# Two-layer graph network on one core: p spread through DRAM, projections one or two strips earlier, both norms scaled on ScalarE

## The chip, the cores and the metric

The kernel runs on one core of one Trainium2 chip. The metric is the device time of one execution in microseconds; the median of several runs is compared. Engines are called by the names of the profile: PE (matrix multiply), PEld (its weight load), DVE or VectorE, ACT or ScalarE, POOL or GpSimd, SP (the queue that issues most DMAs).

## The reference

There are 16 graphs ("batches") of 1024 nodes with 256 features, and two layers. Every layer adds its result to its input and normalises each row.

```python
# layer 0; adj holds 0 and 1 in these inputs, so of the four kinds only e0 is used
e0 = leaky(einsum('bid,bjd->bij', h * a0[:, 0], h))          # leaky slope 0.2
alpha = sigmoid(where(adj == 1, e0, -inf))
x = layernorm(x + einsum('bij,bjd->bid', alpha, h) + bias)
# layer 1
Hh = einsum('bni,io->bno', x, W);  s = Hh @ a_src;  d = Hh @ a_dst
e = where(adj != 0, exp(-leaky_relu(s[:, :, None] + d[:, None, :])), 0)
x = layernorm(x + elu(einsum('bnm,bmo->bno', e, Hh) / rowsum(e)))
```

## The kernel before

A batch is held as 8 tiles of 128 rows. The work of a batch falls into three stages on PE, and the program of each engine is in the order in which the code is written (no scheduler moves anything). In the main loop, iteration `b` does layer 0 of batch `b` and layer 1 of batch `prev = b - 1`, and stores batch `done = b - 2`.

**The strip stage.** Layer 0's scores are symmetric, so only the strips on and above the diagonal are computed: `strip(b, jt)` multiplies (tile `pe`, L198) and has 8, 7, ... 1 blocks of 128 columns for `jt` = 0 to 7. ACT takes two tanh of `pe` (`tb` L206, `low` L207), VectorE takes their maximum (L208), `finish` writes the row of `al` (L214) and POOL adds the diagonal (L224). `tb` has four buffers and `low` two. The lower half comes through DRAM: `dump` turns 32 x 32 blocks on VectorE (L230) and writes `tb` out on SP's queue (`mir`, L234), `gather` reads it back in columns (L238), and `mask(b, t)` on VectorE applies the adjacency to it (L244). Masks 0 to 2 stand after strips 5 to 7, masks 3 to 6 in the first sum. Between the strips stand the eight projections of the batch before: `project(prev, t)` (tile `pH`, L343), from which ACT makes `H` and, by an exponential, the two columns `pq` (L351 to L353), p and q of each node. In the main loop projection `t` stands after strip `t`; for the first batch they stand later.

`spread_p` (L355 to L363) lays p, which is a column, along the free axis on all 128 partitions: for each of eight tiles PE transposes the column repeated 128 times (`pp`, L362), and ACT copies two times 512 columns to `p` (L363).

**The first sum.** `sum0(b, t)`: eight `al` x `x` products for each of eight row tiles (`acc`, L294), then on VectorE the eviction (L302) and the row statistics (`st`, `mv`, L264 and L265). After four tiles POOL computes `r`, the inverse deviation (`rstd`, L271 to L279). VectorE then subtracts the mean and multiplies by `r` (`scale`, L283): for the first four tiles in slots 5 and 6, for the last four in the second sum. The scaled rows go to DRAM and back in blocks (`save_x1`, `fetch_x1`), and `turn_x1` on VectorE (L331) makes of them what `project` reads. In the same slots VectorE makes the weights of layer 1, `weights(prev, t)` (`e`, L375), one of eight per slot: a row tile of `e` from `p`, `q` and the adjacency. `scale1(done, t)` scales a tile of the output on VectorE, also by L283. ACT has four checks of the adjacency here (`junk`, L116). At the end POOL issues the load of a later adjacency (L102).

**The second sum.** `sum1`: eight `e` x `H` products per row tile (`acc`, L382), then `elu` on VectorE and ACT (L397 to L403) and `add` with its statistics on VectorE. The tail, after the loop, ends the last batch; there the output is scaled on ACT instead (`center` and `scale1_act`, L425), with POOL making the product of mean and `r`, negated (`mr`).

`ps_acc`, the pool of `acc` and `pH` in PSUM, has three buffers, `ps_e` of `pe` three, `ps_t` of `pp` two. `p` and `H` have one buffer each.

Of the kernel before, what the change touches and what calls it, by code (L numbers as in the profile page):

```python
# [18 lines left out]
P = 128  # L19
# [10 lines left out]
def one_kind_pass(  # L30
# [236 lines left out]
    def rstd(mv, what):  # L267

        n_t = mv.shape[1]
        ve = small.tile([P, NT], F32, tag="ve", name=f"ve_{what}")[:, 0:n_t]  # L270
        nc.gpsimd.tensor_scalar(ve, mv[:, :, 1], EPS, None, ALU.add)  # L271
        r = small.tile([P, NT], F32, tag="r", name=f"r_{what}")[:, 0:n_t]
        nc.gpsimd.tensor_tensor(r, ve, power[:, 0:n_t], ALU.pow)  # L273

        n = small.tile([P, NT], F32, tag="n", name=f"n_{what}")[:, 0:n_t]
        nc.gpsimd.tensor_tensor(n, r, r, ALU.mult)
        nc.gpsimd.tensor_tensor(n, n, ve, ALU.mult)
        nc.gpsimd.tensor_scalar(n, n, -0.5, 1.5, ALU.mult, ALU.add)
        nc.gpsimd.tensor_tensor(r, r, n, ALU.mult)  # L279
        return r  # L280

    def scale(y, mv, r):
        nc.vector.tensor_scalar(y, y, mv[:, 0:1], r, ALU.subtract, ALU.mult)  # L283

    x1s, mv0s, r0s = {}, {}, {}

    def sum0(b, t):
        if t == 0:
            x1s[b] = two.tile([P, NT, D], F32, tag="x1", name=f"x1_{b}")
            mv0s[b] = small.tile([P, NT, 2], F32, tag="mv0", name=f"mv0_{b}")  # L290
            r0s[b] = {}
        acc = ps_acc.tile([P, D], F32, tag="acc", name=f"acc0_{b}_{t}")
        for jt in range(NT):
            nc.tensor.matmul(  # L294
                acc,
                lhsT=als[b][:, jt, ts(t, P)],
                rhs=xs[b][:, jt, :],
                start=(jt == 0),
                stop=(jt == NT - 1),
            )  # L300
        y = x1s[b][:, t, :]
        nc.vector.scalar_tensor_tensor(y, acc, 0.5, bias_bc, ALU.mult, ALU.add)  # L302
        stats(y, mv0s[b][:, t, :], f"0_{b}_{t}")
        if t % HT == HT - 1:
            g = t // HT
            r0s[b][g] = rstd(mv0s[b][:, ts(g, HT), :], f"0_{b}_{g}")

    def scale0(b, t):
        scale(x1s[b][:, t, :], mv0s[b][:, t, :], r0s[b][t // HT][:, t % HT : t % HT + 1])


    x1Ts, Hs, pqs, p_bcs, es = {}, {}, {}, {}, {}
# [42 lines left out]
    def spread_p(b, g):  # L355

        if g == 0:
            p_bcs[b] = one.tile([P, N], F32, tag="p", name=f"p_{b}")
        pt = ps_t.tile([P, HT, P], F32, tag="t", name=f"pp_{b}_{g}")
        for t in range(HT):  # L360
            col = pqs[b][:, g * HT + t, 0:1]
            nc.tensor.transpose(pt[:, t, :], col.to_broadcast([P, P]), ident)  # L362
        nc.scalar.copy(p_bcs[b][:, ts(g, HALF)], pt.rearrange("p t q -> p (t q)"))  # L363

    def check_pq(b):
        near = small.tile([P, NT, 2], F32, tag="near", name=f"near_{b}")
        nc.vector.tensor_scalar(near, pqs[b], LOW, 1.0 / LOW, ALU.max, ALU.min)
        nc.vector.tensor_tensor(near, near, pqs[b], ALU.is_equal)
        nc.vector.tensor_reduce(fit[:, b : b + 1], near, AX.XY, ALU.min)
# [6 lines left out]
            es[b][:, m, :], p_bcs[b], pqs[b][:, m, 1:2], adjs[b][:, m, :], ALU.mult, ALU.min  # L376
        )

    hs, ys, mv1s, r1s, rms = {}, {}, {}, {}, {}

    def sum1(b, t, acc, m):
        nc.tensor.matmul(  # L382
# [26 lines left out]
        nc.vector.scalar_tensor_tensor(y, y, -1.0, x1s[b][:, t, :], ALU.add, ALU.add)  # L409
        stats(y, mv1s[b][:, t, :], f"1_{b}_{t}")  # L410

    def center(b, t0, n):

        mv = mv1s[b][:, ds(t0, n), :]
        r = rstd(mv, f"1_{b}_{t0}")
        mr = small.tile([P, NT], F32, tag="mr", name=f"mr_{b}_{t0}")[:, 0:n]
        nc.gpsimd.tensor_tensor(mr, mv[:, :, 0], r, ALU.mult)
        nc.gpsimd.tensor_scalar(mr, mr, -1.0, None, ALU.mult)
        for t in range(n):
            rms[b, t0 + t] = r[:, t : t + 1], mr[:, t : t + 1]  # L420

    def scale1_act(b, t):
        y = ys[b][:, t, :]
        r, mr = rms[b, t]
        nc.scalar.activation(y, y, AF.Identity, bias=mr, scale=r)  # L425

    def scale1(b, t):
        scale(ys[b][:, t, :], mv1s[b][:, t, :], r1s[b][:, t : t + 1])

    def store(b, t0, n):  # L430
        rows = out[b].rearrange("(t p) d -> p t d", p=P)
# [2 lines left out]
    def acc1(b, t, pool, tag):  # L434
        return pool.tile([P, D + 1], F32, tag=tag, name=f"acc1_{b}_{t}")
# [36 lines left out]
    for b in range(1, B):  # L472
        prev, done = b - 1, b - 2
        last = b == B - 1

        projects = [[jt] for jt in range(NT)]
        if prev == 0:

            projects = [[], [], [], [0, 1], [2, 3], [], [4, 5], [6, 7]]
        for jt in range(NT):  # L480
            strip(b, jt)
            if prev == 0 and jt in (1, 2):
                scale0(0, 2 * jt + 2)
                scale0(0, 2 * jt + 3)
            if prev == 0 and jt == 2:
                save_x1(0, 1)
                fetch_x1(0, 1)
            if prev == 0 and jt in (2, 5):
                turn_x1(0, (jt - 2) // 3)
            finish(b, jt)  # L490
            if jt < NT - 1:
                dump(b, jt)
            if jt >= 1:
                gather(b, jt - 1)
            for t in projects[jt]:
                project(prev, t)
            if jt >= 5:
                mask(b, jt - 5)
        for g in range(2):
            spread_p(prev, g)  # L500
        check_pq(prev)
        if not last:
            load_x(b + 1)
            new_xT(b + 1)
            load_blocks(xTs[b + 1], x[b + 1], 0, N)

        for t in range(NT):
            if 1 <= t < 5:
                mask(b, t + 2)
            weights(prev, t)  # L510
            if done >= 0:
                scale1(done, t)
                if t in (3, 7):
                    store(done, t - 3, HT)
            sum0(b, t)
            if t in (5, 6):
                scale0(b, 2 * t - 10)
                scale0(b, 2 * t - 9)
            if t == 6:
                save_x1(b, 0)  # L520
            if t >= NT - CHECKS:
                check_adj(b, t - NT + CHECKS)
        if not last:
            load_adj(b + 1)


        for t in range(NT):
            acc = acc1(prev, t, ps_acc, "acc")
            for m in range(NT):
                sum1(prev, t, acc, m)  # L530
            if last and t == 6:
                turn_x1(b, 1)
            if last and t == 7:
                weights(b, 0)
                weights(b, 1)
            elu(prev, t, acc)
            if t >= 1:
                add(prev, t - 1)
            if t == 0:
                fetch_x1(b, 0)  # L540
            if t in (1, 2):
                scale0(b, 2 * t + 2)
                scale0(b, 2 * t + 3)
            if t == 2:
                save_x1(b, 1)
            if t == 4:
                fetch_x1(b, 1)
                turn_x1(b, 0)
            if not last and t in (3, 5):
                turn_x(b + 1, (t - 3) // 2)  # L550
            if last and t in (5, 6):
                for n in range(HT):
                    project(b, (t - 5) * HT + n)
                spread_p(b, t - 5)
        if not last:
            turn_x1(b, 1)
            add(prev, NT - 1)
            r1s[prev] = rstd(mv1s[prev], f"1_{prev}")


    last, done = B - 1, B - 2
    first = [acc1(last, t, ps_e, "e") for t in range(3)]
    for m in range(NT):
        if m >= 2:
            weights(last, m)
        if m == 3:
            add(done, NT - 1)
            center(done, 0, NT)
        for t in range(3):
            sum1(last, t, first[t], m)  # L570
    check_pq(last)
    for t in range(NT):
        if t < 3:
            acc = first[t]
        else:
            acc = acc1(last, t, ps_acc, "acc")
            for m in range(NT):
                sum1(last, t, acc, m)
        elu(last, t, acc)
        if t in (3, 6):  # L580
            center(last, t - 3, 3)
        add(last, t)
        if t == 6:
            center(last, 6, 1)
        for q in range(2 * t - 6, 2 * t - 4) if 3 <= t < 7 else []:
            scale1_act(done, q)
            if q in (3, 7):
                store(done, q - 3, HT)
        if t == 6:
            for q in range(3):  # L590
                scale1_act(last, q)
            store(last, 0, 3)
    for q in range(3, 7):
        scale1_act(last, q)
        if q == 5:
            store(last, 3, 3)
    center(last, 7, 1)
    scale1_act(last, 7)
    store(last, 6, 2)


# [389 lines left out]
```

## Time and profile before

| | |
|---|---|
| median of 3 runs | 1329.43 us (1328.62 to 1329.67) |
| the profiled execution | 1330.3 us, span 1328.4 us, granted clock 0.992 |
| busy: PE, PEld, DVE, ACT, POOL | 1280.3, 1037.4, 1019.5, 546.5, 243.4 us |
| L382, L294, L198, L343 (PE) | 448.7, 448.5, 269.4, 133.0 us |
| L362 `pp` on PE, x128 | 20.5 us busy, mean 280 ns; 14.6 us idle before it |
| L363 copy of `p` on ACT, x32 | 17.1 us, mean 588 ns |
| L375 `e` on DVE, x128 | 162.8 us, mean 1275 ns |
| L283 scalings on DVE, x112 and x128 | 45.6 and 45.3 us, mean 408 and 396 ns |
| L425 scaling on ACT, x16 | 8.6 us, mean 596 ns |
| L102 `adj` issue on POOL, x34 | mean 800 ns; 1024 KB land in 13.6 us (median) |

A group of the page is a line with an engine: how often it ran, its busy time, the mean of one, and the idle time of its engine just before it with what ended that. A matmul's duration of 380 ns is longer than its place on PE, since matmuls are pipelined: 128 of them take 27.64 us in the chain. The chain follows what ended last back from the end; a wait says how long an engine stood, and for whom.

### The profile page before, as it was taken

The numbers are of one execution on the slowest core, as the hardware profiler recorded it, in microseconds if no ns is written. First come the engines' busy times: TensorE is split into PE (matmuls) and PEld (weight loads), VectorE is DVE, ScalarE is ACT, GpSimd is POOL, SyncE is SP. The second block draws the span as 40 slices with busy tenths as digits, with TensorE's granted clock in tenths as the row PEclk, the third lists the DMA queues.
The fourth block names the chain that finished last, engine by engine and source line by source line (L and its number), as shares of the span: only waits on it lengthen the run. The fifth ranks groups of instructions, "written<-read, shape, count | busy, mean of one in ns | idle before, by whom it ended". The sixth has DMA issues, their size and how long they took to land.

```text
span 1328.4 us, 17516 instructions
## 1 busy us (share of the span) xinstructions
PE 1280.3 (96%) x5550; PEld 1037.4 (78%) x5550; DVE 1019.5 (77%) x2318; ACT 546.5 (41%) x1236; POOL 243.4 (18%) x486
## 2 busy tenths in 40 slices
PE   7879999999999999999999999999999999999995
PEld 5758788687887878788687887878778687787874
DVE  5576886968869687886878869687886878869764
ACT  3352452715336162452715336162451624427034
POOL 2111111211112122111211112122111211112113
PEclk9999999999999999999999999999999999999998
DMA  9265687575677756687575677856686565775211
GB/s 215 54 133 113 109 174 143 113 164 104 145 141 157 160 103 150 109 180 143 111 162 106 150 138 152 162 105 151 111 177 130 110 151 106 172 143 111 68 29 66
DMA packets 606516, 173.36 MB, mean 130 GB/s; under 512 B 485584, under 2 KB 590928, under 8 KB 606416
## 3 DMA queue, kind: packets, MB, share of 16 engines
q1 hardware_dynamic: 580144, 137.56, 48.0%
q0 software_dynamic: 17952, 33.56, 14.8%
q10 hardware_dynamic: 8320, 1.05, 0.5%
q8 instruction: 46, 0.75, 0.2%
q14 instruction: 54, 0.44, 0.1%
HBM read 144.57 MB, written 61.08 MB: 155 GB/s over the span
## 4 chain that ended last, share of the span: by engine, by line
PE 83%; DVE 6%; DMA 3%; ACT 3%; SPq 2%; ACTq 1%; issue 1%; POOL 0%; DVEq 0%; POOLq 0%
PE acc L294 32%; PE acc L382 32%; PE pe L198 13%; PE pH L343 5%; DMA mir<-tb 2%; SPq L234 2%; DVE tb L208 1%; DVE al L214 1%; ACTq L110 1%; DVE tb L230 1%; ACT tb L206 1%; PE pp L362 1%; ACT low L207 1%; DVE st L264 1%; DVE y L409 0%
## 5 line engine op out<-in xcount | busy, mean ns | idle before, releaser
L382 PE MATMUL acc<-H,e 128*128 128x257 f32 x2048 | 448.7, 380 | 1.6 <-DVE e L375 1.6
L294 PE MATMUL acc<-x,al 128*128 128x256 f32 x2048 | 448.5, 381 | 0.0
L382 PEld LDWEIGHTS acc<-H,e 128*128 128x128 f32 x2048 | 387.9, 190 | 59.5 <-DVE e L375 2.4
L294 PEld LDWEIGHTS acc<-x,al 128*128 128x128 f32 x2048 | 389.5, 191 | 53.5 <-issue 0.5
L402 ACT ACTIVATE h<-acc,rinv 128x256 f32<-128x256 f32 x128 | 60.2, 470 | 562.2 <-DVE rinv L400 559.3
L198 PE MATMUL pe<-xa,xT 128*128 128x384 f32 (+3 forms) x768 | 269.4, 488 | 0.2 <-ACT low L207 0.2
L198 PEld LDWEIGHTS pe<-xa,xT 128*128 128x128 f32 x768 | 143.3, 191 | 87.5 <-issue 42.6
L271 POOL TENSOR_SCALAR ve<-mv 128x4 f32<-128x4 f32 (+3 forms) x51 | 18.0, 352 | 811.4 <-DVE mv L265 796.7
L375 DVE SCALAR_TENSOR_TENSOR e<-p,pq,adj 128x1024 f32<-128x1024 f32 x128 | 162.8, 1275 | 2.8 <-ACT p L363 2.8
L206 ACT ACTIVATE tb<-pe 128x512 f32<-128x512 f32 (+1 forms) x192 | 94.3, 491 | 136.5 <-PE pe L198 87.2
L343 PE MATMUL pH<-Wx,x1T 128*128 128x258 f32 x512 | 133.0, 386 | 7.1 <-DVE x1T L331 4.2
L343 PEld LDWEIGHTS pH<-Wx,x1T 128*128 128x128 f32 x512 | 97.2, 193 | 43.0 <-issue 17.6
L116 ACT ACTIVATE junk<-adj,minus 128x2048 bf16<-128x2048 bf16 x64 | 128.4, 2007 | 1.5
L397 DVE COPY rs<-acc 128x1 f32<-128x1 f32 x128 | 19.7, 154 | 138.9 <-PE acc L382 138.5
L208 DVE TENSOR_TENSOR tb<-tb,low 128x512 f32<-128x512 f32 (+1 forms) x192 | 99.3, 542 | 28.4 <-ACT low L207 25.8
L224 POOL TENSOR_TENSOR al<-ident,al 128x128 f32<-128x128 f32 x128 | 68.9, 538 | 240.9 <-DVE al L214 240.9
L214 DVE SCALAR_TENSOR_TENSOR al<-tb,adj 128x512 f32<-128x512 f32 (+7 forms) x132 | 99.4, 753 | 4.1
L302 DVE SCALAR_TENSOR_TENSOR x<-acc,bias_bc 128x256 f32<-128x256 f32 x128 | 54.3, 424 | 60.4 <-PE acc L294 59.2
L207 ACT ACTIVATE low<-pe 128x512 f32<-128x512 f32 (+1 forms) x192 | 93.3, 486 | 3.6 <-DVE tb L208 3.5
L273 POOL TENSOR_TENSOR r<-ve,power 128x4 f32<-128x4 f32 (+3 forms) x51 | 78.5, 1539 | 4.3
L230 DVE STREAM_TRANSPOSE tb<-tb 128x896 f32<-128x896 f32 (+6 forms) x105 | 74.7, 712 | 3.6
L244 DVE SCALAR_TENSOR_TENSOR al<-al,adj 128x896 f32<-128x896 f32 (+6 forms) x105 | 72.9, 694 | 0.9 <-DMA al<-mir 0.7
(58 smaller groups left out, 866.3 us busy)
## 6 DMA issues: line engine op xcount, KB each, us to landing
adj<-in_adjT POOLq DMA_DIRECT2D x30, 1024.0 KB, 13.6
x_rows<-x SPq DMA_DIRECT2D x32, 512.0 KB, 3.7
x1T<-x_rows SPq DMA_DIRECT2D x256, 64.0 KB, 2.4
x<-in_x SPq DMA_DIRECT2D x15, 1024.0 KB, 6.2
out<-y SPq DMA_DIRECT2D x30, 512.0 KB, 3.0
xT<-in_x SPq DMA_DIRECT2D x112, 128.0 KB, 3.2
mir<-tb SPq DMA_DIRECT2D x60, 112.0 KB, 2.4
al<-mir SPq DMA_DIRECT2D x15, 448.0 KB, 4.1
```

Of the source, the lines that this page charges most:

```text
L116: nc.scalar.activation(junk, adjs[b][:, ts(n, NT // CHECKS), :], AF.Square, bias=minus1, scale=2.0, accum_out=chk[:, b * CHECKS + n : b * ...
L198: nc.tensor.matmul(pe[:, 0:w], lhsT=xTs[b][:, c, ts(jt, P)], rhs=xas[b][:, c, ds(jt * P + o, w)], start=(c == 0), stop=(c == ND - 1),)
L206: nc.scalar.activation(tb[:, ds(o, w)], pe[:, 0:w], AF.Tanh, scale=0.5)
L207: nc.scalar.activation(low[:, 0:w], pe[:, 0:w], AF.Tanh, scale=0.5 * SLOPE)
L208: nc.vector.tensor_tensor(tb[:, ds(o, w)], tb[:, ds(o, w)], low[:, 0:w], ALU.max)
L214: nc.vector.scalar_tensor_tensor(als[b][:, jt, c0:c1], tbs[b, jt][:, c0 - jt * P : c1 - jt * P], 1.0, adjs[b][:, jt, c0:c1], ALU.add, ALU. ...
L230: nc.vector.transpose(tb, tb)
L273: nc.gpsimd.tensor_tensor(r, ve, power[:, 0:n_t], ALU.pow)
L294: nc.tensor.matmul(acc, lhsT=als[b][:, jt, ts(t, P)], rhs=xs[b][:, jt, :], start=(jt == 0), stop=(jt == NT - 1),)
L343: nc.tensor.matmul(pt, lhsT=x1Ts[b][:, c, ts(t, P)], rhs=Wx[:, c, :], start=(c == 0), stop=(c == ND - 1),)
L375: nc.vector.scalar_tensor_tensor(es[b][:, m, :], p_bcs[b], pqs[b][:, m, 1:2], adjs[b][:, m, :], ALU.mult, ALU.min)
L382: nc.tensor.matmul(acc, lhsT=es[b][:, m, ts(t, P)], rhs=Hs[b][:, m, :], start=(m == 0), stop=(m == NT - 1),)
```

## The change

`share_p` takes the place of `spread_p` in the loop: PE transposes the eight columns of p once to eight rows (8 x 128), ACT copies them, POOL's queue writes the 4 KB to DRAM and then reads them back to all 128 partitions. It stands after strip 6 (for the first batch after the last projection). The projections stand earlier in the strips: 0 and 1 after strip 0, 2 after 1, 3 after 2, 4 and 5 after 3, 6 after 4, 7 after 5. The eight `weights` move from one per slot to slots 2 to 7. `center` is used for both norms: POOL makes `mr` from mean and `r`, and ACT scales with one activation in the places where VectorE scaled. The last batch keeps `spread_p`.

```diff
--- before.py
+++ after.py
@@ -279,8 +279,17 @@
         nc.gpsimd.tensor_tensor(r, r, n, ALU.mult)
         return r
 
-    def scale(y, mv, r):
-        nc.vector.tensor_scalar(y, y, mv[:, 0:1], r, ALU.subtract, ALU.mult)
+    def center(mv, what):
+
+        r = rstd(mv, what)
+        n = mv.shape[1]
+        mr = small.tile([P, NT], F32, tag="mr", name=f"mr_{what}")[:, 0:n]
+        nc.gpsimd.tensor_tensor(mr, mv[:, :, 0], r, ALU.mult)
+        nc.gpsimd.tensor_scalar(mr, mr, -1.0, None, ALU.mult)
+        return [(r[:, t : t + 1], mr[:, t : t + 1]) for t in range(n)]
+
+    def scale(y, r, mr):
+        nc.scalar.activation(y, y, AF.Identity, bias=mr, scale=r)
 
     x1s, mv0s, r0s = {}, {}, {}
 
@@ -288,7 +297,7 @@
         if t == 0:
             x1s[b] = two.tile([P, NT, D], F32, tag="x1", name=f"x1_{b}")
             mv0s[b] = small.tile([P, NT, 2], F32, tag="mv0", name=f"mv0_{b}")
-            r0s[b] = {}
+            r0s[b] = []
         acc = ps_acc.tile([P, D], F32, tag="acc", name=f"acc0_{b}_{t}")
         for jt in range(NT):
             nc.tensor.matmul(
@@ -303,10 +312,10 @@
         stats(y, mv0s[b][:, t, :], f"0_{b}_{t}")
         if t % HT == HT - 1:
             g = t // HT
-            r0s[b][g] = rstd(mv0s[b][:, ts(g, HT), :], f"0_{b}_{g}")
+            r0s[b] += center(mv0s[b][:, ts(g, HT), :], f"0_{b}_{g}")
 
     def scale0(b, t):
-        scale(x1s[b][:, t, :], mv0s[b][:, t, :], r0s[b][t // HT][:, t % HT : t % HT + 1])
+        scale(x1s[b][:, t, :], *r0s[b][t])
 
 
     x1Ts, Hs, pqs, p_bcs, es = {}, {}, {}, {}, {}
@@ -362,6 +371,18 @@
             nc.tensor.transpose(pt[:, t, :], col.to_broadcast([P, P]), ident)
         nc.scalar.copy(p_bcs[b][:, ts(g, HALF)], pt.rearrange("p t q -> p (t q)"))
 
+    def share_p(b):
+
+
+        pt = ps_t.tile([P, HT, P], F32, tag="t", name=f"prow_{b}")[0:NT, 0, :]
+        nc.tensor.transpose(pt, pqs[b][:, :, 0], ident)
+        row = small.tile([NT, P], F32, tag="row", name=f"row_{b}")
+        nc.scalar.copy(row, pt)
+        p_row = dram.tile([N], F32, tag="p_row", name=f"p_row_{b}")
+        nc.gpsimd.dma_start(p_row.rearrange("(t p) -> t p", p=P), row)
+        p_bcs[b] = one.tile([P, N], F32, tag="p", name=f"p_{b}")
+        nc.gpsimd.dma_start(p_bcs[b], p_row.partition_broadcast(P))
+
     def check_pq(b):
         near = small.tile([P, NT, 2], F32, tag="near", name=f"near_{b}")
         nc.vector.tensor_scalar(near, pqs[b], LOW, 1.0 / LOW, ALU.max, ALU.min)
@@ -376,7 +397,7 @@
             es[b][:, m, :], p_bcs[b], pqs[b][:, m, 1:2], adjs[b][:, m, :], ALU.mult, ALU.min
         )
 
-    hs, ys, mv1s, r1s, rms = {}, {}, {}, {}, {}
+    hs, ys, mv1s, r1s = {}, {}, {}, {}
 
     def sum1(b, t, acc, m):
         nc.tensor.matmul(
@@ -409,23 +430,8 @@
         nc.vector.scalar_tensor_tensor(y, y, -1.0, x1s[b][:, t, :], ALU.add, ALU.add)
         stats(y, mv1s[b][:, t, :], f"1_{b}_{t}")
 
-    def center(b, t0, n):
-
-        mv = mv1s[b][:, ds(t0, n), :]
-        r = rstd(mv, f"1_{b}_{t0}")
-        mr = small.tile([P, NT], F32, tag="mr", name=f"mr_{b}_{t0}")[:, 0:n]
-        nc.gpsimd.tensor_tensor(mr, mv[:, :, 0], r, ALU.mult)
-        nc.gpsimd.tensor_scalar(mr, mr, -1.0, None, ALU.mult)
-        for t in range(n):
-            rms[b, t0 + t] = r[:, t : t + 1], mr[:, t : t + 1]
-
-    def scale1_act(b, t):
-        y = ys[b][:, t, :]
-        r, mr = rms[b, t]
-        nc.scalar.activation(y, y, AF.Identity, bias=mr, scale=r)
-
     def scale1(b, t):
-        scale(ys[b][:, t, :], mv1s[b][:, t, :], r1s[b][:, t : t + 1])
+        scale(ys[b][:, t, :], *r1s[b][t])
 
     def store(b, t0, n):
         rows = out[b].rearrange("(t p) d -> p t d", p=P)
@@ -473,7 +479,7 @@
         prev, done = b - 1, b - 2
         last = b == B - 1
 
-        projects = [[jt] for jt in range(NT)]
+        projects = [[0, 1], [2], [3], [4, 5], [6], [7], [], []]
         if prev == 0:
 
             projects = [[], [], [], [0, 1], [2, 3], [], [4, 5], [6, 7]]
@@ -494,10 +500,10 @@
                 gather(b, jt - 1)
             for t in projects[jt]:
                 project(prev, t)
+            if jt == (6 if prev > 0 else 7):
+                share_p(prev)
             if jt >= 5:
                 mask(b, jt - 5)
-        for g in range(2):
-            spread_p(prev, g)
         check_pq(prev)
         if not last:
             load_x(b + 1)
@@ -507,7 +513,8 @@
         for t in range(NT):
             if 1 <= t < 5:
                 mask(b, t + 2)
-            weights(prev, t)
+            for m in ([], [], [0, 1], [2], [3], [4], [5], [6, 7])[t]:
+                weights(prev, m)
             if done >= 0:
                 scale1(done, t)
                 if t in (3, 7):
@@ -555,17 +562,18 @@
         if not last:
             turn_x1(b, 1)
             add(prev, NT - 1)
-            r1s[prev] = rstd(mv1s[prev], f"1_{prev}")
+            r1s[prev] = center(mv1s[prev], f"1_{prev}")
 
 
     last, done = B - 1, B - 2
+    r1s[last] = []
     first = [acc1(last, t, ps_e, "e") for t in range(3)]
     for m in range(NT):
         if m >= 2:
             weights(last, m)
         if m == 3:
             add(done, NT - 1)
-            center(done, 0, NT)
+            r1s[done] = center(mv1s[done], f"1_{done}")
         for t in range(3):
             sum1(last, t, first[t], m)
     check_pq(last)
@@ -578,24 +586,24 @@
                 sum1(last, t, acc, m)
         elu(last, t, acc)
         if t in (3, 6):
-            center(last, t - 3, 3)
+            r1s[last] += center(mv1s[last][:, ds(t - 3, 3), :], f"1_{last}_{t - 3}")
         add(last, t)
         if t == 6:
-            center(last, 6, 1)
+            r1s[last] += center(mv1s[last][:, 6:7, :], f"1_{last}_6")
         for q in range(2 * t - 6, 2 * t - 4) if 3 <= t < 7 else []:
-            scale1_act(done, q)
+            scale1(done, q)
             if q in (3, 7):
                 store(done, q - 3, HT)
         if t == 6:
             for q in range(3):
-                scale1_act(last, q)
+                scale1(last, q)
             store(last, 0, 3)
     for q in range(3, 7):
-        scale1_act(last, q)
+        scale1(last, q)
         if q == 5:
             store(last, 3, 3)
-    center(last, 7, 1)
-    scale1_act(last, 7)
+    r1s[last] += center(mv1s[last][:, 7:8, :], f"1_{last}_7")
+    scale1(last, 7)
     store(last, 6, 2)
 
 
```

## The prediction

> **What bounds the kernel now.** I read the busy shares, then the waits of PE, then the chain that ended last, then VectorE's timeline in one batch. The page's line of busy times:
>
> ```profile
> PE 1280.3 (96%) x5550; PEld 1037.4 (78%) x5550; DVE 1019.5 (77%) x2318; ACT 546.5 (41%) x1236; POOL 243.4 (18%) x486
> ```
>
> and, of the waits of PE (total, times, longest), the largest and the one of the second sum:
>
> ```profile
> PE pp L362 <- ACT pq L352: 14.6, 12, 2.2
> ...
> PE acc L382 <- DVE e L375: 1.6, 2, 1.0
> ```
>
> PE is busy 96% of the span, so only PE's own work and idle time count. Its largest wait by far is that of the `pp` transposes for `pq`. The chain shows a batch without it and the end of one with it (start, length, what):
>
> ```profile
> 552.61 3.43 PE pe L198 x8
> ...
> 569.86 1.29 PE pe L198 x4
> ...
> 574.20 0.88 PE pH L343 x4
> 575.08 1.08 PE pp L362 x8
> 576.15 27.64 PE acc L294 x128
> 603.79 27.85 PE acc L382 x128
> ```
>
> ```profile
> 972.98 2.90 DMA mir<-tb
> ...
> 976.57 0.32 PE pp L362
> ```
>
> I call the stretch from the first `pe` matmul to the first `acc` of L294 the strip stage and count from its start. It took 23.54 us here, 25.80 in the batch from 951.10. In the latter ACT's `tb` of strip 7 waits for the dump of strip 3 (972.98), and `pq` of projection 7 stands behind it in ACT's queue, so PE waits. Over the 14 batches 2 to 15 the chain's stages sum to 344.1 us, mean 24.58; the two sums after them take 27.64 and 27.84 with PE never idle.
>
> ```profile
> 570.14 0.69 DVE L208 TENSOR_TENSOR tb<-tb,low 128x512 f32<-128x512 f32 x1 [0.52 <-ACT low L207]
> ...
> 572.09 0.55 DVE L208 TENSOR_TENSOR tb<-tb,low 128x384 f32<-128x384 f32 x1
> ...
> 573.64 1.08 DVE L244 SCALAR_TENSOR_TENSOR al<-al,adj 128x896 f32<-128x896 f32 x1
> ```
>
> This is the second limit, hidden today: `mask(b,0)` (L244), which the second matmul of the first sum needs, ends at 574.72, offset 22.11, after VectorE has done strips 4 and 5. It starts at 21.02 to 21.04 in each of the seven batches I looked at, the quick and the slow, so it is no part of the difference between them.
>
> **What the Trainium skill says.** "ScalarE: Activation LUTs", What ACT_TABLE_LOAD costs: 186 ns plus 0.833 ns a column, plus about 93 ns for each of two pointer operands. For 256 columns I estimate 585 ns; the trace has 596 (L425). "DMA: Bandwidth & Descriptors", Anatomy of one DMA: from POOL about 2.0 us plus bytes/436e3, an estimate of 3.2 us for 512 KB. The trace doesn't agree where it can be held against it: `adj` of 1024 KB, written from POOL, takes 13.6 us to land (8.6 at least). The same page, Two DMAs through the same engine are not ordered: the issuing engine must wait for the first DMA's semaphore before one that reads its bytes; so POOL stands between the two DMAs of `p`. No DMA pair of POOL in this trace shows it.
>
> **The change, part by part.**
>
> *Spreading p (15 batches; the last keeps the old way).* Removed: 8 transposes, 1.08 us on PE's path, and their wait for `pq`; also two ACT copies of 588 ns. Added: one transpose of 128 columns, 1.08/8 = 0.14 us, an ACT copy of 8 x 128 (0.28 us, the row of a 128-column `tb`) and two POOL DMAs. The transpose stands after strip 6 (0.87 us of matmuls). In the trace `pq` is done 0.45 us after its projection ends (573.59 to 574.05), so it waits for nothing. The waits of strip 7's `tb` no longer touch PE.
>
> *Features up by one or two strips.* No work is added, but the order is: strip 0, two projections (1.74), 1, one, 2, one, 3, two, 4, one, 5, one, 6, transpose, 7. With the chain's lengths (3.43, 3.01, 2.58, 2.15, 1.72, 1.29, 0.87, 0.44 and 0.87 each) PE is through at 22.60. That is 23.54 - 1.08 + 0.14. But six projections instead of four now precede strip 4, seven instead of five precede strip 5. Strip 4 ends at 18.12, was 16.37; strip 5 at 20.28, was 18.54. VectorE gets `low` of strip 4 1.13 us later, at 19.25, then needs 3.50 us to the mask (570.14 to 573.64). By strip 5: 20.28 + 0.91 + 1.58 = 22.77. Both give **22.77 for the mask's start, 23.85 for its end**. PE has one matmul pair (0.43) to do before it, so the sum starts in effect at 23.85 + 0.05 - 0.43 = **23.47**, 0.87 later than PE could. `mask(b,1)` ends 3.23 after the first one's start, at 26.0, and is needed at 27.4; the later ones have more. New wait per batch: PE for VectorE's mask.
>
> Gain: 24.58 - 23.47 = 1.11 us, times 14 = **15.5 us**.
>
> *POOL and p's arrival.* `row` waits behind the diagonal of strip 6, which follows the mask: 23.85 + 0.85 + 0.5 = 25.2. Issue 0.8 (L102), landing of 4 KB 2.2 (the small `mir` rows, 1.9 to 2.3), issue 0.8: 29.0. Landing of 512 KB: 3.0 and 3.7 us in `out` and `x_rows`, 8.6 in the fastest `adj`; I take 4, so p is there at 33. What is queued behind it on POOL, the diagonal of strip 7, is needed in the eighth sum. On VectorE the first `e` would be reached at 32.0 (second `acc` at 30.4, its three instructions 1.05, a mask 0.53). It waits 1 us, with the eviction of `acc` 2 and masks 5 and 6 behind it. Three `acc` buffers cover that: the sixth sum, at 40.8, needs the buffer evicted at p + 3.0, so PE stops only if p comes after **37.8**. The last `e` is done at p + 16 and needed at 54.1: the same bound. Price 0 (no gain is hidden there either, since PE doesn't wait for L375's `e` in these batches now), and 15 us for every us beyond the bound. SP's queue is passed by nothing new, but its gathers for masks 4 to 6 are in flight beside p: 15 x 0.5 MB are added to 173 MB. A late gather holds up VectorE as a late p does, under the same bound.
>
> *Scalings.* VectorE loses 16 of 0.40 us a batch in the sums, where PE doesn't wait for it: no gain. The last `mask` chain begins with strip 0, and at its start VectorE already idles 1.47 us before the last `rs`, so nothing reaches it. ACT gains 16 of 0.60 = 9.6 us against 9.3 us busy of 27.64 in the first sum and 8.0 of 27.84 in the second. In order, its squares of `adj` (2.2 each) now stand behind scalings that wait for POOL's chain. I put them through: the fourth sum is evicted at 39.5 (p at 33, then `e` 0 and 1, `acc` 2, a mask, `e` 2, `acc` 3: 6.5); POOL's chain to `mr` takes 4.2 (3.3 in the trace from 591.21, with 0.9 for two operations and gaps), so the first scaling starts at 43.7. Then two scalings (1.1), a square (2.2), three scalings (1.6), a square, one scaling, a square: 53.6. The first `acc` of the second sum is there at 54.6, so the cover is 1 us, and behind it the three buffers. The saved rows of the first half leave at 48.6 where they left at 50.6 (save of x1 in SP's queue), so the second norm's input is no later. POOL gains two operations of 0.24 a group. Price 0; at most about 1 us a batch if ACT ran late by three sums.
>
> *Batch 1.* ACT's scalings displace a square into an idle stretch (52 to 59.8) and leave VectorE's chain to the strip-1 dump 0.7 shorter; I take -1.0 (from -2 to +2). `pp` there stands after the last projection before and after. The tail keeps its work: 0.
>
> Sum: 15.5 + 1.0 = 16.5. The profiled execution took 1330.3 (span 1328.4 and 1.9 around it), so 1313.8; the median shown is 0.9 lower: **1312.9, I say 1313**. One first sum took 29.33 us at a clock of 0.94; I leave that in. Own range 1308 to 1319: the mask's end is good to 0.3 us, times 14.
>
> **The rivals.**
> *The mask isn't the limit* (0.13). If VectorE caught up, PE would start at 22.60: 14 x 1.98 = 27.7 and 1.0, about 1301. For it: the waits name only `pq`. Against: the six equal offsets of the mask.
> *p or ACT somewhat late* (0.17). p at 38.3, half a us past the bound, gives 7 us back: 1320; up to 1 us gives 1328.
> *p far too late: slower* (0.12). Each us past 37.8 costs 15. It eats the whole gain when p's second DMA lands after 37.8 + 1.1 - 29.0 = 9.9 us. With the median of `adj`, 13.6 us, PE would stand 4.8 us a batch, 72 us: 1385. For it: `adj` is the only row of POOL's DMAs, and DMA share is 0.73 to 0.78 between 576 and 588. Against: half the bytes, and rows of 4 KB where the others' are mostly under 512 B.
> *That the change doesn't do what it says* is excluded by the instruction order: 15 single transposes in place of 15 times 8.
>
> **How the numbers follow.** Mine 0.58. Range 1300 to 1328 takes in the first two rivals and leaves out the slower one and a little below. A run can tell about 0.2%, 2.7 us, from no change. Faster 0.84, same 0.04, slower 0.12.
>
> **What would show it.** Right: no `pp` of the first 15 batches, strip stages near 23.5 and all alike, a new PE wait for VectorE's `al` (L244) of about 0.9 x 14 = 12 us, the `e` wait for p about 1 us, no PE wait for `e`. Wrong: stages of 22.6 (the mask), or PE waiting for L375's `e` or for evictions (p).

## The result, and the profile after

The changed kernel takes **1319.43 us** (median of 4 runs, 1318.28 to 1320.1) where the kernel before took 1329.55 (4 runs, 1328.62 to 1332.45): a ratio of 0.9922, interval 0.9908 to 0.9936. The profiled execution took 1320.1 us with a span of 1318.0. The prediction said 1313, with a range from 1300 to 1328: faster, as forecast, by some 10 us rather than 16. Its narrower range, 1308 to 1319, which rested on the mask's end alone, is just missed.

The page's busy times of the kernel after:

```profile
PE 1271.8 (96%) x5445; PEld 1025.8 (78%) x5445; DVE 938.2 (71%) x2078; ACT 650.6 (49%) x1461; POOL 302.9 (23%) x608
```

PE has 105 instructions fewer, which is 15 times seven transposes. VectorE lost 81 us of busy time and ACT gained 104. The shares say no more than that: PE is still busy 96% of a shorter span. The waits say where the time went. First PE's own, then PE's weight load (PEld), VectorE's for p, and POOL's (total, times, longest):

```profile
PE acc L303 <- DVE al L244: 12.7, 14, 0.9
...
PE prow L378 <- ACT pq L361: 0.3, 1, 0.3
```

```profile
PEld acc L303 <- DVE al L244: 18.3, 14, 1.3
```

```profile
DVE e L396 <- DMA p<-p_row: 9.3, 11, 2.0
```

```profile
POOL p L384 <- DMA p_row<-row: 38.9, 15, 3.9
```

The wait for `pq`, 14.6 us before, is gone: the single transpose waits once, in the first batch. In its place stands the wait for the mask, once in each of 14 batches, 0.9 us each. POOL's wait for its own first DMA holds up nothing that PE needs.

The stages of a batch, from the starts of the first `pe`, the first `acc` of the first sum and the first `acc` of the second in PE's timeline:

| us | before | after |
|---|---|---|
| strip stage | 23.54 to 25.79 | 22.58, all 14 alike |
| first sum | 27.64 (once 29.33) | 28.80, all 14 alike |
| second sum | 27.84 | 27.84 |
| batch to batch | 79.02 to 82.96 | 79.22 |

A quick batch before was *faster* than any batch after (79.02 against 79.22). The gain comes from the batches that waited for `pq`.

The timelines of PE, of its weight loads and of VectorE at the border of the first sum in one batch, whose strip stage starts at 630.01 (start, length, what; in brackets the idle time before it):

```profile
652.04 0.27 PE L378 MATMUL prow<-ident,pq 128*8 128x128 f32 x1
652.14 0.61 PE L198 MATMUL pe<-xa,xT 128*128 128x128 f32 x4
652.59 0.60 PE L303 MATMUL acc<-x,al 128*128 128x256 f32 x2
654.09 3.07 PE L303 MATMUL acc<-x,al 128*128 128x256 f32 x13 [0.90 <-DVE al L244]
```

```profile
652.48 0.30 PEld L303 LDWEIGHTS acc<-x,al 128*128 128x128 f32 x2
654.09 2.89 PEld L303 LDWEIGHTS acc<-x,al 128*128 128x128 f32 x14 [1.30 <-DVE al L244]
```

```profile
649.46 0.69 DVE L208 TENSOR_TENSOR tb<-tb,low 128x512 f32<-128x512 f32 x1 [1.86 <-ACT low L207]
...
652.96 1.08 DVE L244 SCALAR_TENSOR_TENSOR al<-al,adj 128x896 f32<-128x896 f32 x1
```

PE is through with the strips, does the one pair of matmuls that needs no mask, and stops. The mask runs from 652.96 to 654.04, and at 654.09 the load and the matmul start together. VectorE was late because `low` of strip 4 came late: it stood idle 1.86 us before it. From that strip's maximum to the mask it needs 3.50 us, as it did before.

### The profile page after: what moved, and what is told of

Same layout as the page of the kernel before. It is cut to its first block, busy times and chain, and to the rows that moved or that the text cites. A ratio compares the mean times of both kernels' runs of the same rounds, so it can differ in the third digit from the quotient of the medians.

```text
span 1318.0 us, 17487 instructions
## 1 busy us (share of the span) xinstructions
PE 1271.8 (96%) x5445; PEld 1025.8 (78%) x5445; DVE 938.2 (71%) x2078; ACT 650.6 (49%) x1461; POOL 302.9 (23%) x608
## 5 line engine op out<-in xcount | busy, mean ns | idle before, releaser
L303 PE MATMUL acc<-x,al 128*128 128x256 f32 x2048 | 451.9, 381 | 12.7 <-DVE al L244 12.7
L292 ACT ACTIVATE x<-x,mr,r 128x256 f32<-128x256 f32 x128 | 69.4, 593 | 236.3 <-POOL mr L288 236.3
L396 DVE SCALAR_TENSOR_TENSOR e<-p,pq,adj 128x1024 f32<-128x1024 f32 x128 | 159.7, 1270 | 12.3 <-DMA p<-p_row 9.3
L352 PE MATMUL pH<-Wx,x1T 128*128 128x258 f32 x512 | 130.0, 389 | 5.2 <-DVE x1T L340 3.0
L224 POOL TENSOR_TENSOR al<-ident,al 128x128 f32<-128x128 f32 x128 | 60.5, 476 | 221.4 <-DVE al L214 221.1
```

The source lines that it names most:

```text
L303: nc.tensor.matmul(acc, lhsT=als[b][:, jt, ts(t, P)], rhs=xs[b][:, jt, :], start=(jt == 0), stop=(jt == NT - 1),)
L352: nc.tensor.matmul(pt, lhsT=x1Ts[b][:, c, ts(t, P)], rhs=Wx[:, c, :], start=(c == 0), stop=(c == ND - 1),)
L396: nc.vector.scalar_tensor_tensor(es[b][:, m, :], p_bcs[b], pqs[b][:, m, 1:2], adjs[b][:, m, :], ALU.mult, ALU.min)
```

## The experiments

Each is compared with the kernel before on its own chip: 1328.44 us (1324.38 to 1332.88) for the first four, 1330.22 us (1326.9 to 1333.46) for the last four.

### The mask one place earlier

The changed kernel, with `mask(b,0)` in front of the work on strip 5.

```diff
-            if jt >= 5:
-                mask(b, jt - 5)
+            if jt in (4, 6, 7):
+                mask(b, {4: 0, 6: 1, 7: 2}[jt])
```

> The changed kernel with one edit: mask 0 stands after strip 4 on VectorE instead of after strip 5. Theory (the first sum waits 0.9 us for mask 0 and loses another 0.27 us when it starts again): mask 0 ends near 22.3, before PE is through with the strip stage at 22.6; no PE wait for L244 is left, strip stage 22.6, first sum 27.64 instead of 28.80, period 78.06 instead of 79.22, 14 x 1.16 = 16 us faster than the changed kernel: 1303 to 1304. Rival (another wait, mask 1 or a gather, stands right behind it): period 78.8 to 79.2, 1313 to 1319.

Measured: **1302.28 us** (1302.06 to 1303.6), ratio 0.9803 (0.9787 to 0.9818). All 14 batches have 22.58, 27.63 and 27.84, together 78.05. PE's waits no longer have a line for L244. In the chain of one batch the strips now run straight into the sum:

```profile
403.83 1.72 PE pe L198 x4
405.55 0.87 PE pH L352 x4
406.42 1.29 PE pe L198 x4
...
410.00 27.63 PE acc L303 x128
```

In the changed kernel the chain enters the sum from VectorE, one pair of matmuls in:

```profile
1049.06 1.09 DVE al L244
1050.19 27.46 PE acc L303 x126
1077.65 27.84 PE acc L403 x128
```

So the mask is what bounds the changed kernel between strips and sum, and it costs 1.17 us a batch (79.22 less 78.05). VectorE didn't get faster here, it does the same work in another order: what was late was one instruction, not the engine. This version beats both kernels.

### The projections alone

The kernel before, with the new order of the projections; eight transposes and VectorE's scalings stay.

```diff
-        projects = [[jt] for jt in range(NT)]
+        projects = [[0, 1], [2], [3], [4, 5], [6], [7], [], []]
```

> The kernel before with only the new order of the projections; p is spread by the eight transposes as before, the scalings stay on VectorE. Theory (the gain is the removed wait for pq, and the eight transposes now stand where PE would wait for mask 0 anyway): transposes done at 23.54, mask 0 ends at 23.9, one pair of matmuls covers the rest; period 79.0, no PE wait for pq nor for L244 over 1 us in all: 1315 to 1317, some 3 us faster than the whole change. Rival (the gain is that of the single transpose through DRAM): 1326 or more.

Measured: 1317.88 us (1316.55 to 1318.42), ratio 0.9916 (0.9902 to 0.993). The interval is nearly that of the whole change. The stages are 23.34, 28.04 and 27.84: another split, and 79.22 to the digit, the period of the whole change. PE's and PEld's waits:

```profile
PE pp L362 <- ACT pq L352: 0.2, 1, 0.2
```

```profile
PEld acc L294 <- DVE al L244: 7.6, 14, 0.5
```

PE itself shows no wait for L244 in this run, and still each first sum takes 0.40 us longer than 27.64: the time is lost, but only the weight load shows it.

The mask starts 22.94 us after the first `pe` here (650.82 less 627.88), 22.95 in the changed kernel. The seven transposes that the full change saves turn into seven transposes' worth of waiting for it. The order of the projections is therefore all of the gain in this kernel. I had put this run at 1315 to 1317, some 3 us below the full change, and that was wrong: I left out the cost of the restart after the mask, which both pay.

### The single transpose alone

The kernel before, with `share_p` after the last projection in place of `spread_p`, and `weights` in slots 2 to 7.

```diff
+            if jt == 7:
+                share_p(prev)
...
-        for g in range(2):
-            spread_p(prev, g)
...
-            weights(prev, t)
+            for m in ([], [], [0, 1], [2], [3], [4], [5], [6, 7])[t]:
+                weights(prev, m)
```

> The kernel before with only the single transpose and the way through DRAM (after the last projection) and the later slots of the weights; projections and scalings as before. Theory: the single transpose waits for the same pq of projection 7, behind the tb of strip 7, as the last of the eight did, so strip stages of 23.3 to 25.8 stay and the time is 1326 to 1330. Rival (the seven transposes saved are worth 0.94 us a batch by themselves): 1315 to 1317.

Measured: 1330.66 us (1327.75 to 1335.38), ratio 1.0017 (1.0004 to 1.003).

```profile
PE prow L369 <- ACT pq L352: 23.5, 15, 2.8
```

The wait for `pq` was 14.6 us with eight transposes and is 23.5 with one: most of the work removed came back as waiting in front of the transpose that is left, since the projections stand where they stood and `pq` of the last one comes no earlier. In the two profiles the 14 strip stages are 3.4 us shorter in sum (344.1 and 340.7). The first sums take back 2.2 of it, most of that in two sums of 29.38 and 29.19 at granted clocks of 0.94 and 0.95. Over all runs there is no gain, and if anything a loss of 0.2%.

### The scalings alone

The kernel before, with both norms scaled on ACT (`center` and `scale` as in the diff above).

```diff
-        nc.vector.tensor_scalar(y, y, mv[:, 0:1], r, ALU.subtract, ALU.mult)
+        nc.scalar.activation(y, y, AF.Identity, bias=mr, scale=r)
```

> The kernel before with only the scalings of both norms on ACT. Theory (VectorE has slack in both sums, ACT too): 1327.5 to 1331.5, no difference. Rival (VectorE's 6.4 us a batch are part of the gain): 1325 or less. Second rival (ACT in order, squares behind scalings, holds up the second sum): 1333 or more, with PE waits before L403.

Measured: 1328.21 us (1325.9 to 1331.21), ratio 1.0 (0.9989 to 1.0011). VectorE's busy time falls from 1019.5 us to 941.0, and the kernel's time doesn't move.

### Eight transposes, mask early

The projections' order and the early mask together, with `spread_p` and VectorE's scalings.

```diff
-        projects = [[jt] for jt in range(NT)]
+        projects = [[0, 1], [2], [3], [4, 5], [6], [7], [], []]
...
-            if jt >= 5:
-                mask(b, jt - 5)
+            if jt in (4, 6, 7):
+                mask(b, {4: 0, 6: 1, 7: 2}[jt])
```

> The kernel before with the new order of the projections and mask 0 after strip 4; p is spread by the eight transposes, scalings on VectorE. Theory (the single transpose saves PE 0.9 us a batch, which shows only where PE doesn't stand for mask 0): no wait for L244; strip stage 23.3 to 23.5, first sum 27.64, period 78.8 to 79.0, against 78.05 with the single transpose: 10 to 13 us slower than that kernel, 1313 to 1315. Rival (the single transpose is worth nothing anywhere): 1302 to 1304.

Measured: 1311.32 us (1309.71 to 1311.74), ratio 0.9861 (0.9842 to 0.9881); 23.34, 27.63 and 27.84, period 78.81. With the mask out of the way the single transpose is worth 78.81 - 78.05 = 0.76 us a batch. The run came out below the 1313 to 1315 that I expected: I had put the transposes at 0.9 or so, from the 1.08 us of the eight in the chain before; there PEld waits 0.23 us for `pq` among them. Without that wait the eight take 0.88 us of PE (650.34 to 651.22 in the timeline of the projections alone), and 0.88 less one eighth is 0.77.

### Mask early, scalings on VectorE

The first experiment, with the loop's scalings put back on VectorE; ACT keeps the tail's.

```diff
-        nc.scalar.activation(y, y, AF.Identity, bias=mr, scale=r)
+        nc.vector.tensor_scalar(y, y, m, r, ALU.subtract, ALU.mult)
```

> The changed kernel with mask 0 after strip 4 and the scalings of both norms in the loop back on VectorE. Theory (the scalings are hidden on either engine): 1301 to 1305, as with mask 0 early and the scalings on ACT. Rival (with the weights pushed into slots 2 to 7 VectorE has 17.6 us of work there without scalings and 21.7 with them, for 20.7 us of PE): the last e comes late, PE waits before L403 and for evictions, 1 us or more a batch: 1316 or more.

Measured: 1302.96 us (1302.0 to 1304.19), ratio 0.9804 (0.9785 to 0.9824), period 78.05. Even in the fastest version it makes no difference where the norms are scaled.

### p one hop later

The changed kernel, with the row of p copied once more through DRAM by POOL's queue.

```diff
+        for hop in range(1):
+            p_next = dram.tile([N], F32, tag=f"p_hop{hop}", name=f"p_hop{hop}_{b}")
+            nc.gpsimd.dma_start(p_next.rearrange("(t p) -> t p", p=P), p_row.rearrange("(t p) -> t p", p=P))
+            p_row = p_next
```

> The changed kernel with the 4 KB of p copied once more inside DRAM by POOL's queue before they are spread, so that p arrives later by about 2.7 us (issue 0.56, landing about 2.1): offset 34.8 in the batch instead of 32.1. Theory (three acc buffers and the late weights cover p until about 38): no difference to the changed kernel, 1318 to 1321. Rival (PE feels every us that p is late): 40 us more, 1358.

Measured: 1323.23 us (1319.2 to 1325.19), ratio 0.9945 (0.9928 to 0.9963). VectorE's waits:

```profile
DVE e L400 <- DMA p<-p_hop: 60.8, 15, 6.0
```

VectorE stands four us a batch for p, and the first sum is still 28.80 in 13 of 14 batches, with the first `e` 35.4 to 37.7 us into the batch. In the other it came at 38.6, just past the predicted bound (37.8, which is 38.0 by the timeline). There PE waited 0.3 us for an eviction, and the sum took 29.33. Up to the bound the three `acc` buffers do cover a late p.

The time is above the 1318 to 1321 that I expected, and those 3 us or so lie elsewhere. The profiled run was the slowest of the eight, with a span 5.4 us longer than the changed kernel's. In it five of the strip stages grew, by 0.12 to 0.91, together 2.5 us, and from the start of the last activation to the end it took 9.2 us instead of 6.6. In two places PE waited for ACT's `xa`, 1.1 us in all; what stretched the rest I have not settled.

### p three hops later

The same with `range(3)`.

```diff
+        for hop in range(3):
```

> The changed kernel with p copied three more times inside DRAM, so that it arrives about 8 us later, offset 40.2. Theory: past the bound of 38 by some 2 us, PE waits for evictions and for e, 1.5 to 3.5 us a batch, 15 batches: 1340 to 1370. Rival (there is more slack than I counted): 1318 to 1321. Second rival (every us counts): 1440.

Measured: 1435.65 us (1432.85 to 1440.37), ratio 1.0813 (1.0781 to 1.0845). That is far above the 1340 to 1370 that I expected and near the second rival's 1440, but that rival's reason is excluded: with one hop p came 3 to 4 us later and 13 of 14 first sums didn't feel it. The first `e` came 40.8 to 45.6 us into the batch, not at the 40.2 that I had counted on, because the third hop took 5.0 to 6.4 us to land in 12 of 15 batches. The waits of PE and of PEld, and PE and VectorE in one batch (strip stage from 592.05):

```profile
PE acc L303 <- DVE x L311: 79.2, 15, 7.2
```

```profile
PEld acc L303 <- DVE x L311: 85.2, 15, 7.6
```

```profile
616.13 17.10 PE L303 MATMUL acc<-x,al 128*128 128x256 f32 x78 [0.90 <-DVE al L244]
639.36 13.54 PE L303 MATMUL acc<-x,al 128*128 128x256 f32 x48 [6.13 <-DVE x L311]
```

```profile
636.49 2.48 DVE L400 SCALAR_TENSOR_TENSOR e<-p,pq,adj 128x1024 f32<-128x1024 f32 x2 [12.04 <-DMA p<-p_hop]
638.89 0.42 DVE L311 SCALAR_TENSOR_TENSOR x<-acc,bias_bc 128x256 f32<-128x256 f32 x1
```

PE stops after 80 matmuls, at the sixth sum, for the eviction that stands behind two `e`, as the prediction's bound had it: p plus 2.9 us. With p at 44.4 and the bound at 38.0 on this clock (37.8 in the chain's), 6.4 us were due. PE's idle is 6.1, but the batch grew by 9.3 (88.53 against 79.22). The last 48 matmuls show the rest: 13.4 us where 48 of 128 at 27.64 are 10.4. The granted clock in the stretch before the stop and in the one after it (window, length, busy times, PEclk, DMA share, GB/s):

```profile
616.10:633.20 17.10, 17.07 (x78) 14.74 (x78) 6.70 (x18) 4.61 (x8) 3.64 (x7) 1.00 0.81 166
639.40:652.70 13.30, 13.30 (x48) 11.26 (x49) 11.82 (x22) 4.26 (x7) 5.23 (x8) 0.78 0.00 1
```

The sum of PE's idle over the kernel, 79.2 us, is therefore less than the 116 us that it lost. The lower clock didn't come in every batch: in two, after waits of 3.54 and 2.44 us, it stayed at 1.00. One of them:

```profile
203.16 10.63 PE L303 MATMUL acc<-x,al 128*128 128x256 f32 x48 [3.54 <-DVE x L311]
```

## Why the prediction was right or wrong

**The bound and its move: right.** PE's path gave up the wait for `pq`, and the mask that lay hidden behind it set the start of the first sum. Both halves are shown: the single transpose alone keeps the first wait and gains nothing, and moving the mask alone takes the new wait away and gives 14 times 1.17, some 16 us. The rival that the mask isn't the limit, at 1301, is what the early mask made of the kernel. The prediction counts the batches with the same offset of the mask once as seven and once as six; the trace has it in all 14 (21.20 or 21.21 in the timeline's count).

**The strips and the mask: right to 0.02 us.** PE through at 22.60, measured 22.58. The mask was to start at 22.77 in the chain's count, which begins 0.16 later than the timeline's; there it starts at 22.79. The new wait was put at 12 us and is 12.7. One of the prediction's signs was badly chosen: by its own definition the strip stage ends at the first `acc`, which stands before the wait, so the stages measure 22.58 and not 23.5. It had named 22.6 as the sign that the mask is no limit. The wait for L244 and the 28.80 of the first sum show that it is.

**The start of the sum: the term that was mis-sized.** The prediction went from the mask's end to the sum by 0.05 - 0.43: a gap, less the pair of matmuls already done. By the chain the 126 remaining matmuls take 27.46 us, and 126/128 of 27.64 is 27.21. So a restart costs 0.25 more than the pace of a running sum says; with 0.02 of the mask's start the sum begins 0.27 later in effect. Over 14 batches that is **3.8 us**. How it divides is a reading of the trace, which no run took apart. In a running sequence a matmul's end overlaps the next one, and the chain therefore starts a sum 0.16 after the timeline does (576.15 against 575.99 before); after a wait there is nothing to overlap with. The other 0.09 is about the lead of a weight load over its matmul (652.48 against 652.59); after the wait both start at 654.09 and the lead is lost.

That the awaited `al` is the weight operand is not what costs it. In three sums of the runs with hops PE stood for the eviction of an `acc` buffer instead, at a clock of 1.00, for 0.27, 2.44 and 3.54 us. These sums are 0.53, 2.71 and 3.81 longer than 28.80, so they too lost 0.26 or 0.27 beyond the wait. PEld shows more of the loss than PE: its wait is 0.40 longer (1.30 and 0.90 here, 85.2 and 79.2 for 15 waits with three hops). In the projections alone PEld waits 0.54, PE doesn't wait at all, and the sum is 0.40 longer.

**Batch 1: the -1.0 was wrong.** Its second sum began 126.84 us into the span, 1.98 later than before. But ACT's `tb` of strip 6 of batch 0, ahead of anything that the change touches, was already 1.76 later (47.30 against 45.54), in a stretch where the granted clock was lower than before (0.84 against 0.92 from 25 to 47 us). In the first four experiments that sum began at 124.71 to 125.26, and before at 124.86. Of the later ones it began at 125.23 with eight transposes, and late again with the scalings on VectorE (126.18) and with one hop (126.63). So the gain of 1.0 isn't there. Most of the 2.0 was lost before the change acts; whether it has a part in the rest is open.

**The sum, put right.** Predicted gain 16.5 of the span; the 14 strip stages and first sums fell by 13.5 (732.8 to 719.3), which is 15.5 less 3.8, and 1.7 for the one long first sum before that the prediction had left in. That 1.7 is luck: it made up for a part of the miss. Less 2.0 in batch 1, less 1.1 at the end of the span (from the start of the last activation to the end 6.65 us, 5.58 before; put at 0) is 10.4, the difference of the spans, 1328.4 and 1318.0.

**p's arrival: right.** The first DMA is issued at 25.3 (said 25.2). From the start of its issue the 4 KB took 2.1 to 4.1 us to land, median 2.7 (said 0.8 and 2.2). The page's row of the second DMA (KB, median us to landing) says 4.4 (said 0.8 and 4):

```profile
p<-p_row POOLq DMA_DIRECT2D x15, 512.0 KB, 4.4
```

The first `e` stood at 32.3 to 34.4 (33), 11 times after a wait of up to 2.0 us, and PE never waited for it in the loop. The Trainium skill's fit for a DMA from POOL ("DMA: Bandwidth & Descriptors", Anatomy of one DMA) gave 3.2 us as an estimate; the trace, with 4.1 to 5.0, is above it, and the measurement decides. The bound was tested from both sides: with the first `e` at 35.4 to 37.7 (one more hop) the first sum didn't move, with 38.6 PE stopped for 0.3 us, and with 40.8 to 45.6 it stopped at the sixth sum as the rival of the late p had said. Its price, 15 us for each us, was too low: it left out the granted clock after the stop, and the restart.

**The scalings: right at 0.** They are hidden in both orders and on both engines. The order on ACT was also right: in batches 2 to 14 its first scaling starts 43.9 to 45.5 us into the batch (said 43.7), and its last square ends at 52.9 to 54.5 (said 53.6). ACT's group is as the skill's formula had it ("ScalarE: Activation LUTs", What ACT_TABLE_LOAD costs; 585 ns estimated):

```profile
L292 ACT ACTIVATE x<-x,mr,r 128x256 f32<-128x256 f32 x128 | 69.4, 593 | 236.3 <-POOL mr L288 236.3
```

Its 236 us of waiting for POOL look like a new bottleneck and are none: ACT is early.

## What to carry to other kernels

Before removing a wait, find what would be waited for next and time it from the trace in the batches that don't wait: here the equal offsets of one mask named the new bound to 0.02 us. They also point to the remedy, one instruction moved one place up in the order of its engine. Taking work off the critical engine is worth nothing while it waits at a later point anyway (seven transposes: 0 with the mask late, 0.76 us a batch with it early). Count a restart on top of every wait that PE takes on, and look at PEld's waits too: in the projections alone PE shows no wait for the mask, and 0.40 us a batch are lost to it.

## What the runs showed of the hardware

- A wait of PE costs some 0.25 us beyond the wait that its timeline shows. For a weight operand it is 0.25 against the pace of a running sum (27.46 for 126 matmuls, 27.21 at pace), for a PSUM buffer 0.26 or 0.27 in three sums at a clock of 1.00. PEld's wait is 0.40 longer than PE's (1.30 and 0.90).
- After PE had stood 6.1 us, its granted clock was 0.78 over the next 13.3 us, and 48 matmuls took 3 us longer. With three hops the mean clock from the stop to the end of the sum was 0.78 to 0.87 in 13 of 15 batches, after waits of 2.96 to 7.25 us, and 1.00 after waits of 2.44 and 3.54. After the waits of 0.9 us in the changed kernel it stayed at 1.00.
- Of small DMAs of 4 KB that POOL issued one after the other, each waiting for the one before, the second copy between DRAM tiles landed in 1.7 to 3.8 us, and the third in 5.0 to 6.4 us in 12 of 15 batches (1.9 to 2.9 in the others). In the batch shown the DMA engines were busy 41% of the time during the second and all of it during the third. That this load is the cause isn't shown: in one batch the third landed in 2.5 us with the engines just as busy.
